# Key order for contiguous value weights in a two-layer attention kernel

## Chip, cores and metric

The kernel runs on one core of a Trainium2 chip. The metric is the device time of one execution in microseconds (us); where runs are compared, it is the median. The profile is of one execution. Everything is computed in float32.

## What is computed

The input x has shape (4, 32, 32, 768): four images of 1024 tokens and 768 channels. Two layers follow each other. Each normalises its input over 32 groups of channels, computes multi-head attention with 12 heads of 64 channels and a decomposed relative-position bias, projects the result and adds it to the input.

```python
def _gn(v, G=32, eps=1e-5):            # over height, width and the group's channels
    g = v.reshape(B_, H_, W_, G, C_ // G)
    return ((g - m) / jnp.sqrt(s + eps)).reshape(v.shape)
# attention of one layer, S = 1024 tokens
qkv = x @ Wqkv                          # layer 1 adds qkv_b
rel_h = jnp.einsum('bhwc,hkc->bhwk', r_q, Rh)
rel_w = jnp.einsum('bhwc,wkc->bhwk', r_q, Rw)
bias = rel_h[..., :, None] + rel_w[..., None, :]
attn = jax.nn.softmax(scale * jnp.einsum('bqc,bkc->bqk', q, k) + bias, axis=-1)
out = jnp.einsum('bqk,bkc->bqc', attn, v)
x = x + (out @ Wproj + bproj)
```

A key token has a row y and a column x, its number being 32y + x. Its bias is the sum of a row entry and a column entry. The softmax and the weighted sum over keys do not depend on the order of the keys, as long as scores, biases and values use the same one.

## The kernel before

**Units.** There are 8 images (4 for each layer) of 6 head pairs, so 48 head pairs `g`, and each has 8 steps `n` of 128 query tokens. Channels lie on the partitions in x (`xn`, six chunks of 128), queries and keys; tokens do in values.

**Work of a head pair.** `project_in` (L201) multiplies the normalised input by the query and key weights, 512 tokens at a time: ScalarE copies one half of the sum out of PSUM and VectorE (DVE) adds the other (L226 to L229). `project_values` (L236) does the values of two head pairs in four quarters; there the weights that TensorE loads are tokens of `xn`, 128 for one of 8 planes, and the rows that stream are the weight matrix (L248 to L252). `positions` (L268) multiplies queries with the tables of relative positions, and `diagonals` (L294) reads the needed entries back from DRAM into `rel`.

**Work of a step.** `biases` (L311) adds row and column entries on GpSimd (POOL) into a tile `sc` of 128 queries x 1024 keys, two steps ahead. `scores` (L321) multiplies queries by keys, subtracts in one VectorE instruction (L337) with the row's extreme, and takes the exponential on ScalarE (L341). `divide` (L346) rescales on GpSimd (L351). `turn` (L353) transposes 32 x 32 blocks on VectorE (L365) and writes them to DRAM (`td`); `read_back` (L373) fetches them as `pt`, with the keys on the partitions. Each of the 8 planes `k` of `pt` holds 128 keys. `weigh` (L381) multiplies the planes of `pt` with those of the values, twice a head pair. The order of keys decides which tokens a plane holds: before, keys stand in order 32x + y, and a plane holds every eighth token, so L250 takes its weights at a step of eight elements.

**Order.** All of it is one program written out by hand (`manual_schedule`). In each step `biases`, `scores`, `turn` and `divide` come at fixed places, and slices of projections for the next head pair and of the output projection fill the rest: `take` (L516) takes `shares[n]` slices of a list `todo`. A slice of the output projection (`project_out`, L462) is one matmul of 512 columns; a group of one to three slices ends with an eviction on VectorE (L481, L483). An fp32 matmul stands as two instructions in the trace. `early` and `later` hold calls that are issued one or two steps on, and `fetch` (L422) asks for output weights and residuals, four parts ahead. Loads and stores go through the queue of SyncE (SPq), save that ScalarE's queue (ACTq) writes `tdr` (L287) and, at the end, asks for the last `pt`. The group statistics of an image (`norm`, L156) pass through DRAM four times in small transfers: gather (L170), by_group (L173), back (L186) and spread (L189).

**PSUM.** Scores have two tiles (`ps_s`), everything else shares two others (`ps_m`), so a third group waits for the eviction of the first.

Of the kernel before, what the change touches and what calls it, by code (L numbers as in the profile page):

```python
# [36 lines left out]
P = 128  # L37
# [17 lines left out]
def attention_blocks(ctx: ExitStack, tc: tile.TileContext, a: dict, out: bass.AP):  # L55
# [100 lines left out]
    def norm(im):  # L156

        per = dram2.tile([C, 2], FP, tag="per", name=f"per_{im}")
        back = dram2.tile([C, 2], FP, tag="back", name=f"back_{im}")
        g = small.tile([NG, 2, GS, 2], FP, tag="g", bufs=1, name=f"g_{im}")
        st = small.tile([NG, 2, 6], FP, tag="gst", bufs=1, name=f"gst_{im}")
        mv = small.tile([NG, 3, 2], FP, tag="gmv", bufs=1, name=f"gmv_{im}")
        nrm = small.tile([P, NC, 2], FP, tag="nrm", bufs=2, name=f"nrm_{im}")

        def gather():
            nc.sync.dma_start(out=per.rearrange("(c p) s -> p c s", p=P), in_=mv_of[im])  # L170

        def by_group():
            nc.sync.dma_start(out=g[:, 0, :, :], in_=per.rearrange("(g k) s -> g k s", k=GS))  # L173

        def groups():
            for k in range(2):
                nc.vector.bn_stats(st[:, k, :], g[:, 0, :, k])
                nc.vector.bn_aggr(mv[:, k, :], st[:, k, :])
            nc.vector.tensor_scalar(mv[:, 2, 0:1], mv[:, 0, 1:2], mv[:, 1, 0:1], EPS, ALU.add, ALU.add)
            nc.scalar.activation(mv[:, 2, 1:2], mv[:, 2, 0:1], AF.Sqrt)  # L180

        def inverses():
            nc.vector.reciprocal(mv[:, 2, 0:1], mv[:, 2, 1:2])
            for k, x in enumerate((mv[:, 0, 0:1], mv[:, 2, 0:1])):
                nc.vector.tensor_copy(g[:, 1, :, k], x.to_broadcast([NG, GS]))
            nc.sync.dma_start(out=back.rearrange("(g k) s -> g k s", k=GS), in_=g[:, 1, :, :])  # L186

        def spread():
            nc.sync.dma_start(out=nrm, in_=back.rearrange("(c p) s -> p c s", p=P))  # L189
# [11 lines left out]
    def project_in(g, which, i):  # L201
# [16 lines left out]
                yield True  # L218
        to, t = qk_of[g, which], [t[:, a, :] for a in range(2)]
        if which == 1:  # L220
            to = to.rearrange("p (x y) -> p x y", x=HW)[:, :, i * HW // 2 : (i + 1) * HW // 2]
            t = [x.rearrange("p (y x) -> p x y", x=HW) for x in t]
        else:
            to = to[:, cols]
        if images[im][0] == 0:
# [10 lines left out]
    def project_values(g, i):  # L236
# [7 lines left out]
        for k in range(2):  # L244
            for c in range(NC):
                for a in range(2):
                    rows = slice(a * D, (a + 1) * D)
                    nc.tensor.matmul(  # L248
                        t[:, a, k, :],
                        lhsT=xn[c][rows, :].rearrange("p (m k) -> p k m", k=NT)[:, 2 * i + k, :],  # L250
                        rhs=w[rows, c, :], start=(c == 0), stop=(c == NC - 1),
                    )  # L252
                if c % 2 and (k, c) != (1, NC - 1):
                    yield True
# [56 lines left out]
    def biases(g, n):  # L311
        rel = rel_of[g]
        for h in range(2):
            sc = scpool.tile([P, HW, HW], FP, tag="sc", name=f"sc_{g}_{n}_{h}")
            sc_of[g, n, h] = sc
            nc.gpsimd.tensor_tensor(  # L316
                sc, rel[:, h, 1, n, :].unsqueeze(2).to_broadcast([P, HW, HW]),
                rel[:, h, 0, n, :].unsqueeze(1).to_broadcast([P, HW, HW]), ALU.add,
            )

    def scores(g, n):  # L321
# [11 lines left out]
        st = small.tile([P, 3, 2], FP, tag="sm", name=f"sm_{g}_{n}")  # L333
        st_of[g, n] = st
        for h in range(2):
            sc = sc_of[g, n, h].rearrange("p x y -> p (x y)")
            nc.vector.tensor_tensor_reduce(  # L337
                out=sc, in0=ps[h], in1=sc, scale=-scale, scalar=BIG, op0=ALU.add, op1=ALU.min,
                accum_out=st[:, 0, h : h + 1],
# [6 lines left out]
    def divide(g, n):  # L346
        st = st_of[g, n]
        nc.vector.reciprocal(st[:, 2, :], st[:, 1, :])  # L348
        for h in range(2):
            sc = sc_of[g, n, h].rearrange("p x y -> p (x y)")  # L350
# [22 lines left out]
    def read_back(g, quarter, h, td, queue=None):  # L373
# [1 line left out]
        pt_of[g, quarter, h] = pt  # L375
        (queue or nc.sync).dma_start(
            out=pt.rearrange("p r k t -> p r (k t)"),
            in_=td.rearrange("(r j) (y t) -> (j y) r t", r=4, y=4),
        )

    def weigh(g, quarters):  # L381
# [80 lines left out]
    def project_out(im, p, o, i):  # L462
# [26 lines left out]
        elif p == 2:  # L489
            nc.sync.dma_start(out=dst, in_=to)  # L490
        if i == 1 and (im, p, o, i) in place:
            (early if end else later).append(lambda: fetch(place[im, p, o, i] + 4))
        yield True


# [38 lines left out]
    with tc.manual_schedule(engines=ENGINES):  # L534
# [23 lines left out]
        for at, (g, n) in enumerate(units):  # L558
            im, pair = divmod(g, NP)
            end = im + 1 == NI  # L560
            if n == 0:
# [66 lines left out]
        take(todo, len(todo))  # L628

# [54 lines left out]
```

## Time and profile before

Time before: 3565.82 us median of 3 runs (3563.49 to 3567.86). The profiled execution took 3565.2 us. A row of the group table gives the busy time of all instructions of one line and kind, and the mean of one; PE is TensorE's matmuls and PEld its weight loads, which overlap them.

| line, engine | what | count | busy us | mean ns |
|---|---|---|---|---|
| L213 PE | query and key projection | 4608 | 1031.1 | 591 |
| L328 PE | scores | 3072 | 751.6 | 597 |
| L394 PE | weighted sum of values | 6144 | 687.4 | 381 |
| L248 PE | value projection | 4608 | 567.8 | 398 |
| L470 PE | output projection | 1080 | 477.3 | 598 |
| L316 POOL | bias sums | 768 | 1457.0 | 1918 |
| L351 POOL | rescaling | 768 | 852.0 | 1122 |
| L337 DVE | score minus bias | 768 | 909.6 | 1221 |
| L365 DVE | transposes | 768 | 909.9 | 1221 |
| L341 ACT | exponential | 768 | 879.1 | 1145 |

Matmuls overlap each other, so a busy time is less than count times mean. The DMA queue of SyncE keeps the 16 DMA engines busy for 81.8% of the span, that of ScalarE 4.2%.

### The profile page before, as it was taken

How to read it: one execution, taken by the hardware profiler on the slowest of the kernel's cores; microseconds unless marked ns; L12 is line 12 of the kernel's file. 1: busy time of each engine (PE TensorE's matmuls, PEld its weight loads, DVE VectorE, ACT ScalarE, POOL GpSimd, SP SyncE). 2: the span in 40 equal slices, each digit the busy share in tenths (PEclk: the TensorE clock that was granted, in tenths of full speed). 3: DMA queues.
4: the chain of work that ended last, by engine and by line, in shares of the span. 5: the costliest groups of instructions: out<-in, count | busy, mean ns of one | idle time of the engine just before them, and what ended most of it. 6: DMA issues, size and time to landing. Idle time of an engine off the chain costs nothing.

```text
span 3565.2 us, 55101 instructions
## 1 busy us (share of the span) xinstructions
PE 3515.4 (99%) x21120; PEld 2044.5 (57%) x21120; DVE 2381.5 (67%) x3676; ACT 1226.5 (34%) x2040; POOL 2297.6 (64%) x1546
## 2 busy tenths in 40 slices
PE   6999999999999999999999999999999999999998
PEld 4555565555655565556555565556555565556553
DVE  3676767767677666666766666666766667666665
ACT  2334333333333333333333333333333333333331
POOL 3767666666666666666666666666666666666663
PEclk9999999999999999999999999999999999999999
DMA  4889988998989888998989888898889898888886
GB/s 134 309 319 309 328 296 315 325 309 306 323 313 319 306 318 296 320 318 285 332 301 329 304 294 321 317 320 290 315 315 321 302 306 321 311 311 281 305 281 242
DMA packets 624856, 1084.53 MB, mean 304 GB/s; under 512 B 247120, under 2 KB 310096, under 8 KB 575440
## 3 DMA queue, kind: packets, MB, share of 16 engines
q1 hardware_dynamic: 570672, 1028.31, 81.8%
q10 hardware_dynamic: 53920, 52.70, 4.2%
q8 instruction: 166, 2.72, 0.3%
q14 instruction: 98, 0.80, 0.1%
HBM read 580.59 MB, written 500.27 MB: 303 GB/s over the span
## 4 chain that ended last, share of the span: by engine, by line
PE 96%; DMA 2%; DVE 1%; issue 0%; SPq 0%; ACT 0%; POOL 0%; DVEq 0%; ACTq 0%
PE pj L213 28%; PE s L328 19%; PE av L394 19%; PE pv L248 15%; PE o L470 14%; PE tp L280 3%; DMA tdr<-t 1%; DMA pt<-td 0%; DMA td<-tb 0%; DMA wv<-in_wv 0%; DVE tb L365 0%; SPq L306 0%; DVE sc L337 0%; DMA per<-mv 0%; SPq L94 0%
## 5 line engine op out<-in xcount | busy, mean ns | idle before, releaser
L351 POOL TENSOR_SCALAR sc<-sc,sm 128x1024 f32<-128x1024 f32 x768 | 852.0, 1122 | 1174.2 <-DVE sm L348 1161.0
L316 POOL TENSOR_TENSOR sc<-rel 128x1024 f32<-128x1024 f32 x768 | 1457.0, 1918 | 40.9 <-DMA rel<-tdr 40.9
L341 ACT ACTIVATE sc<-sc,sm 128x1024 f32<-128x1024 f32 x768 | 879.1, 1145 | 1377.8 <-DVE sm L337 1375.5
L337 DVE CUSTOM_DVE_ANT_0 sc<-s,sc 128x1024 f32<-128x1024 f32 x768 | 909.6, 1221 | 292.9 <-PE s L328 256.9
L213 PE MATMUL pj<-xn,w 64*128 64x512 f32 x4608 | 1031.1, 591 | 29.7 <-DVE xn L192 27.4
L365 DVE STREAM_TRANSPOSE tb<-sc 128x1024 f32<-128x1024 f32 x768 | 909.9, 1221 | 19.9 <-DMA td<-tb 19.0
L213 PEld LDWEIGHTS pj<-xn,w 64*128 64x128 f32 x4608 | 453.8, 188 | 568.7 <-issue 534.2
L328 PE MATMUL s<-k,q 64*128 64x512 f32 x3072 | 751.6, 597 | 7.4 <-DVE sm L337 7.3
L394 PE MATMUL av<-pt,v 128*64 128x256 f32 x6144 | 687.4, 381 | 4.6 <-DMA pt<-td 4.4
L394 PEld LDWEIGHTS av<-pt,v 128*64 128x64 f32 x6144 | 433.9, 137 | 287.6 <-ACT v L258 35.6
L248 PEld LDWEIGHTS pv<-wv,xn 64*128 64x128 f32 x4608 | 570.2, 331 | 31.1 <-DVE v L259 9.9
L248 PE MATMUL pv<-wv,xn 64*128 64x256 f32 x4608 | 567.8, 398 | 0.0
L470 PE MATMUL o<-attn,wo 128*128 128x512 f32 x1080 | 477.3, 598 | 0.0
L328 PEld LDWEIGHTS s<-k,q 64*128 64x128 f32 x3072 | 299.4, 188 | 291.3 <-issue 264.7
L470 PEld LDWEIGHTS o<-attn,wo 128*128 128x128 f32 x1080 | 202.2, 191 | 272.6 <-issue 262.1
L259 DVE TENSOR_TENSOR v<-pv,v 128x256 f32<-128x256 f32 x192 | 81.5, 424 | 320.3 <-ACT v L258 320.3
L258 ACT COPY v<-pv 128x256 f32<-128x256 f32 x192 | 71.4, 372 | 380.6 <-PE pv L248 333.0
L285 ACT COPY t<-tp 128x1024 f32<-128x1024 f32 x96 | 97.2, 1012 | 249.2 <-PE tp L280 147.5
L341 ACT ACTIVATION_READ_ACCUMULATOR sc<-sc,sm 128x1 f32 x768 | 143.3, 187 | 0.0
L229 DVE TENSOR_TENSOR q<-pj,q 128x512 f32<-128x512 f32 x96 | 66.3, 691 | 105.1 <-ACT q L226 53.5
L229 DVE TENSOR_TENSOR k<-pj,k 128x512 f32<-128x512 f32 x96 | 66.1, 689 | 92.8 <-ACT k L226 46.7
L280 PEld LDWEIGHTS tp<-tab,q 64*128 64x128 f32 x1536 | 100.1, 188 | 40.0 <-issue 39.9
(34 smaller groups left out, 788.2 us busy)
## 6 DMA issues: line engine op xcount, KB each, us to landing
td<-tb SPq DMA_DIRECT2D x384, 1024.0 KB, 5.9
pt<-td SPq DMA_DIRECT2D x382, 1024.0 KB, 7.7
tdr<-t ACTq DMA_DIRECT2D x96, 512.0 KB, 6.4
w<-in_wqk SPq DMA_DIRECT2D x96, 384.0 KB, 7.1
rel<-tdr SPq DMA_DIRECT2D x760, 32.0 KB, 2.2
part<-res SPq DMA_DIRECT2D x84, 256.0 KB, 5.1
res<-part SPq DMA_DIRECT2D x84, 256.0 KB, 9.2
wv<-in_wv SPq DMA_DIRECT2D x24, 768.0 KB, 8.7
```

Of the source, the lines that this page charges most:

```text
L213: nc.tensor.matmul(t[:, a, :], lhsT=w[rows, c, :], rhs=xn[c][rows, cols], start=(c == 0), stop=(c == NC - 1),)
L229: nc.vector.tensor_tensor(to, t[1], to, ALU.add)
L248: nc.tensor.matmul(t[:, a, k, :], lhsT=xn[c][rows, :].rearrange("p (m k) -> p k m", k=NT)[:, 2 * i + k, :], rhs=w[rows, c, :], start=(c == ...
L280: nc.tensor.matmul(ps[:, h, j, :], lhsT=q[rows, at * P : (at + 1) * P], rhs=tabs[l][rows, :], start=True, stop=True,)
L316: nc.gpsimd.tensor_tensor(sc, rel[:, h, 1, n, :].unsqueeze(2).to_broadcast([P, HW, HW]), rel[:, h, 0, n, :].unsqueeze(1).to_broadcast([P, ...
L328: nc.tensor.matmul(ps[h][:, cols], lhsT=q[rows, n * P : (n + 1) * P], rhs=k[rows, cols], start=True, stop=True,)
L337: nc.vector.tensor_tensor_reduce(out=sc, in0=ps[h], in1=sc, scale=-scale, scalar=BIG, op0=ALU.add, op1=ALU.min, accum_out=st[:, 0, h : h + 1],
L341: nc.scalar.activation(sc, sc, AF.Exp, bias=st[:, 0, h : h + 1], scale=-1.0, accum_out=st[:, 1, h : h + 1],)
L351: nc.gpsimd.tensor_scalar(sc, sc, st[:, 2, h : h + 1], 1.0, ALU.mult, ALU.mult)
L365: nc.vector.transpose(tb[:, :, j, :], sc_of[g, n, h])
L394: nc.tensor.matmul(av[rows, at * 2 * P : (at + 1) * 2 * P], lhsT=v_of[g][:, k, rows], rhs=pt_of[g, quarter, h][:, :, k, :], start=(k == 0) ...
L470: nc.tensor.matmul(t, lhsT=wo_of[im, o, c], rhs=attn_of[im * NP + c][:, cols], start=(c == c0), stop=(c == c1 - 1),)
```

## The change

The keys are put into another order. `project_in` writes key token 4m + a to place 256a + m, with a from 0 to 3. A plane of `pt` then holds 128 neighbouring tokens, and `project_values` takes `xn` as it lies. `biases` makes its sums in the same order: place 256a + 8(k u) + l has row (k u) and column 4l + a, so the row entry is held over 8 elements while the column entries are read in runs of 8 at a step of four elements; before, the column entry was held over 32 while 32 row entries were read in a run.

Beside it, the first image's statistics go through ScalarE's queue; in the last image a load is issued where its slot becomes free and not a step later; and in the last head pair the slices are shared out differently, with some of them before the transposes, and the twelve that are left over run ahead of the last two weightings.

```diff
@@ norm
+        queue = nc.sync if im else nc.scalar
         def gather():
-            nc.sync.dma_start(out=per.rearrange("(c p) s -> p c s", p=P), in_=mv_of[im])
+            queue.dma_start(out=per.rearrange("(c p) s -> p c s", p=P), in_=mv_of[im])
...
@@ project_in
         if which == 1:
-            to = to.rearrange("p (x y) -> p x y", x=HW)[:, :, i * HW // 2 : (i + 1) * HW // 2]
-            t = [x.rearrange("p (y x) -> p x y", x=HW) for x in t]
+            to = to.rearrange("p (a m) -> p a m", a=4)[:, :, i * P : (i + 1) * P]
+            t = [x.rearrange("p (m a) -> p a m", a=4) for x in t]
@@ project_values
-                        lhsT=xn[c][rows, :].rearrange("p (m k) -> p k m", k=NT)[:, 2 * i + k, :],
-                        rhs=w[rows, c, :], start=(c == 0), stop=(c == NC - 1),
+                        lhsT=xn[c][rows, (2 * i + k) * P : (2 * i + k + 1) * P], rhs=w[rows, c, :],
+                        start=(c == 0), stop=(c == NC - 1),
@@ biases
+            shape = [P, 4, HW, 8]
             nc.gpsimd.tensor_tensor(
-                sc, rel[:, h, 1, n, :].unsqueeze(2).to_broadcast([P, HW, HW]),
-                rel[:, h, 0, n, :].unsqueeze(1).to_broadcast([P, HW, HW]), ALU.add,
+                sc.rearrange("p (a k) (u l) -> p a (k u) l", a=4, l=8),
+                rel[:, h, 0, n, :].unsqueeze(1).unsqueeze(3).to_broadcast(shape),
+                rel[:, h, 1, n, :].rearrange("p (l a) -> p a l", a=4).unsqueeze(2).to_broadcast(shape),
+                ALU.add,
             )
@@ project_out
         if i == 1 and (im, p, o, i) in place:
-            (early if end else later).append(lambda: fetch(place[im, p, o, i] + 4))
+            if end:
+                fetch(place[im, p, o, i] + 4)
+            else:
+                later.append(lambda: fetch(place[im, p, o, i] + 4))
@@ the loop over units, last head pair of the last image
-                        shares = [0, 6, 6, 6, 6, 2, 0, 4]
+                        shares = [6, 6, 0, 6, 6, 2, 0, 4]
...
-            if n == NT - 1:
-                take(todo, share // 4)
-                share -= share // 4
+            first = 3 if n == NT - 1 else 2 if end and pair == NP - 1 and n in (3, 4) else 0
+            first = min(first, share)
+            take(todo, first)
+            share -= first
             turn(g, n)
@@ after the loop
-        run(early)
-        run(later)
-        weigh(NPAIR - 1, (2,))
-        while todo:
-            take(todo, 1)
-            run(early)
-            run(later)
-        weigh(NPAIR - 1, (3,))
+        take(todo, 12)
+        for quarter in (2, 3):
+            weigh(NPAIR - 1, (quarter,))
```

The other three transfers of the statistics change queue in the same way, and the softmax's views are renamed without moving anything.

More of the change, by code (lines that the diff above doesn't have):

```diff
@@ L167, in norm @@
         nrm = small.tile([P, NC, 2], FP, tag="nrm", bufs=2, name=f"nrm_{im}")
+        queue = nc.sync if im else nc.scalar
         def gather():
-            nc.sync.dma_start(out=per.rearrange("(c p) s -> p c s", p=P), in_=mv_of[im])
+            queue.dma_start(out=per.rearrange("(c p) s -> p c s", p=P), in_=mv_of[im])
         def by_group():
-            nc.sync.dma_start(out=g[:, 0, :, :], in_=per.rearrange("(g k) s -> g k s", k=GS))
+            queue.dma_start(out=g[:, 0, :, :], in_=per.rearrange("(g k) s -> g k s", k=GS))
         def groups():
@@ L185, in inverses @@
                 nc.vector.tensor_copy(g[:, 1, :, k], x.to_broadcast([NG, GS]))
-            nc.sync.dma_start(out=back.rearrange("(g k) s -> g k s", k=GS), in_=g[:, 1, :, :])
+            queue.dma_start(out=back.rearrange("(g k) s -> g k s", k=GS), in_=g[:, 1, :, :])
         def spread():
-            nc.sync.dma_start(out=nrm, in_=back.rearrange("(c p) s -> p c s", p=P))
+            queue.dma_start(out=nrm, in_=back.rearrange("(c p) s -> p c s", p=P))
         def apply(c):
@@ L335, in scores @@
         for h in range(2):
-            sc = sc_of[g, n, h].rearrange("p x y -> p (x y)")
+            sc = sc_of[g, n, h].rearrange("p k j -> p (k j)")
             nc.vector.tensor_tensor_reduce(
@@ L349, in divide @@
         for h in range(2):
-            sc = sc_of[g, n, h].rearrange("p x y -> p (x y)")
+            sc = sc_of[g, n, h].rearrange("p k j -> p (k j)")
             nc.gpsimd.tensor_scalar(sc, sc, st[:, 2, h : h + 1], 1.0, ALU.mult, ALU.mult)
@@ L377, in read_back @@
             out=pt.rearrange("p r k t -> p r (k t)"),
-            in_=td.rearrange("(r j) (y t) -> (j y) r t", r=4, y=4),
+            in_=td.rearrange("(r j) (a t) -> (j a) r t", r=4, a=4),
         )
```

## Prediction

> **What bounds the kernel now.** I read the page's busy shares first, then the chain that ended last, then the groups of instructions, then TensorE's timeline in the middle, at the start and at the end.
>
> ```profile
> PE 3515.4 (99%) x21120; PEld 2044.5 (57%) x21120; DVE 2381.5 (67%) x3676; ACT 1226.5 (34%) x2040; POOL 2297.6 (64%) x1546
> ...
> PE 96%; DMA 2%; DVE 1%; issue 0%; SPq 0%; ACT 0%; POOL 0%; DVEq 0%; ACTq 0%
> ```
>
> TensorE is busy 99% and carries 96% of the chain. In the chain in order of time, one output-projection block comes round at 1053.15, 1125.95 and 1198.74 us: one head pair every 72.79 us, 48 of them. So time goes where TensorE's stream gets shorter, provided nobody else needs more than about 72 us a head pair. The groups say which blocks can shrink:
>
> ```profile
> L213 PEld LDWEIGHTS pj<-xn,w 64*128 64x128 f32 x4608 | 453.8, 188 | 568.7 <-issue 534.2
> L248 PEld LDWEIGHTS pv<-wv,xn 64*128 64x128 f32 x4608 | 570.2, 331 | 31.1 <-DVE v L259 9.9
> L248 PE MATMUL pv<-wv,xn 64*128 64x256 f32 x4608 | 567.8, 398 | 0.0
> ```
>
> (The third field after the first bar is the idle time before them.) The two weight loads have one shape, 64 rows by 128 columns. That of the value projection takes 331 ns, not 188, and the weight-load path is hardly ever idle before it (31.1 us over 4608, against 568.7): these matmuls follow their weight loads. The only difference in the code is that L250 picks every eighth token (a step of 32 bytes), where L214 reads 128 neighbours.
>
> ```profile
> 1017.10 5.32 PE L213 MATMUL pj<-xn,w 64*128 64x512 f32 x24
> 1022.25 1.88 PE L328 MATMUL s<-k,q 64*128 64x512 f32 x8
> ...
> 1029.12 5.90 PE L248 MATMUL pv<-wv,xn 64*128 64x256 f32 x48
> 1034.80 1.93 PE L328 MATMUL s<-k,q 64*128 64x512 f32 x8
> ```
>
> Start to next start, a query/key block of 24 x 512 columns takes 5.15 us; a value block of 48 x 256, the same number of columns, takes 5.68 (5.73 in layer 1, where one runs from 3431.30 to 3437.03).
>
> [...]The trace has 188 ns for all loads of 128 neighbouring columns (L213, L280, L328) and 331 for the stepped one.[...]
>
> **The change, part by part.**
>
> *Value weights contiguous (L250).* 24 groups of two head pairs x 4 quarters = 96 blocks. A block cannot go below the 5.15 us of the block with equal columns. It has 24 instructions more; the relative-position block (1004.62 to 1005.52 us, 16 instructions of 128 columns) needs 0.056 us an instruction, of which 128 columns at 5.15/(24x512) = 0.42 ns are 0.0536, so 0.0025 us an instruction, 0.06 a block at most. That block also shows that 188 ns loads keep up at one per 56 ns; the value block needs one per 107. So 5.15 to 5.21; I take 5.19 against a mean of 5.71: 0.52 x 96 = **50 us** (48 to 54). Nothing lies beside it that has to end first: TensorE never stops between 119 us and the last head pair.
>
> *Key order, softmax, transposes, reads back (L221, L336, L350, L378).* Same shapes and sizes. The key eviction reads PSUM at a step of 4 elements instead of 32 and writes runs of 128 instead of 16. Before, the stepped k eviction (ACT 584, DVE 689 ns) costs what the plain q one does (585, 691), so I take 0, hidden under TensorE anyway. Scores and the DRAM round trip have the same patterns: 0.
>
> *Bias sums (L316), 768 on GpSimd.* The row input was contiguous; now the column input is read in runs of 8 at a step of 16 bytes, against a broadcast row entry. Not in this trace: lower bound 1918 ns, unchanged.[...] I take 2.8 as an estimate. Upper bound: double, if the runs of 8 cost as well, 3.8. GpSimd now needs 16 x (1918 + 1122 ns) = 48.6 us of 72.8 a head pair; at 2.8 it needs 62.8, still under TensorE's 71.75. Step by step: its idle times before L351 in one head pair are 0.91, 1.79, 3.94, 1.16, 6.34, 1.90, 4.35 and 4.77 us, and two sums become 1.8 us longer, so a rescale comes at most 0.9 us later. In the timelines the rescaled tile waits some 2 us or more for its transpose: rescale ended 1024.43, transposes began 1026.82, behind the scores' reduction. A sum made at 1006.76 to 1010.54 is first read at 1017.41. So hidden, except at the start: the first two sums (from 58.65 us) stand before the first reduction, **+1.4 us** (0 to 1.8), and about 2 at the very end, counted below.
>
> *First group statistics on ScalarE's queue.*
>
> ```profile
> 13.43 0.21 DVE L154 BATCH_NORM_AGGREGATE mv<-st 128x2 f32<-128x12 f32 x1
> 13.74 0.33 SPq L139 DMA_DIRECT2D bqkv<-in_bqkv  x1
> 15.75 0.38 SPq L170 DMA_DIRECT2D per<-mv  x1
> ```
>
> The statistics are there at 13.64, but the gather goes out at 15.75, and the queue's waits name the landing of wv for it. In a queue of its own it goes at about 13.7. The chain behind it (20.02, 23.10, 24.44, normalising at 26.50, first matmul 27.37) keeps its lengths: **-2 us** (0 to 2.5). Behind the gather on ScalarE stand only L180, which needs its result, and the first eviction at 35.65: no one waits longer. For images 1 to 7 nothing changes.
>
> *Last head pair.* Starts of the score blocks in steps 0 to 6 of before: 3465.76, 3469.16, 3480.88, 3495.46, 3504.85, 3514.23, 3518.06. These 52.3 us hold six score blocks (1.9 each), 26 output slices (24 instructions are 12 slices in 10.5 us, so 0.875) and one weighting of 7.06: 41.2 us of work, 11.1 lost. Step 0 has nothing to fill it while the scores wait for DVE to empty their PSUM tile; in steps 3 and 4 the third group waits 1.86 and 1.84 for DVE:
>
> ```profile
> 3469.16 4.92 PE L328 MATMUL s<-k,q 64*128 64x512 f32 x8 [1.41 <-DVE sm L337]
> ...
> 3502.94 1.99 PE L470 MATMUL o<-attn,w_last 128*128 128x512 f32 x4 [1.86 <-DVE sum L483]
> ...
> 3534.98 5.35 PE L394 MATMUL av<-pt,v 128*64 128x256 f32 x30 [2.45 <-DMA pt<-td]
> ```
>
> The new shares fill step 0 (step 2 has the weighting to fill it), and two slices ahead of the transposes let DVE empty one group before them: I give back 9 of 11.1, since DVE needs some 6.6 us of the 7.15 of such a step. After step 7, 3527.76 to 3561.4 = 33.6 us hold 22 slices (19.3), two half weightings (7.1) and one eviction (0.6): 6.7 lost, mostly waiting for pt (0.45 + 2.45 and a slow stretch after it). Twelve slices (10.5 us) ahead of both weightings cover the first pt. The last pt was asked for at 3540.0 and takes 7.7 to land; with three slices before the last transposes it comes some 1.5 us later, and the slower bias sum adds 2, so some of it shows: 4 back. **-13 us** in all (6 to 18). The fetch in place makes the sync queue wait for a residual buffer with td writes and pt reads behind it; 0, since a DVE eviction frees it within a group of three slices (2.6 us), and the queue's waits show td writes held up 52 times, by up to 2.9 us, without TensorE waiting.
>
> Sum: 3565.8 - 50 + 1.4 - 2 - 13 = 3502.2 us.
>
> **The rivals.** *GpSimd becomes the bound.* It passes 72.8 us a head pair at 72.8/16 - 1.12 = 3.43 us a sum, between my bounds. At 3.8 it needs 16 x 4.92 = 78.7: 48 x 78.7 + 58.7 before its first sum + some 30 after its last rescale = 3866 us, slower by 8%. For it: runs of 8, a read never seen here, and the engine already at 64%.[...] Chance 12%. *GpSimd shows in part*, at 3.1 to 3.4 us a sum: 67 to 72 us a head pair, with short steps in which it no longer catches up; a third to three quarters of the gain goes, 3520 to 3550. Chance 10%. *The loads stay slow* (331 ns is not the step but a conflict on xn): only the edges remain, 3565.8 - 13.6 = 3552. Against it: q, read as weights at 128 neighbours, takes 188. Chance 4%. *DMA becomes the bound*: its share in the middle, 0.85 to 0.89, becomes 0.86 to 0.90, and the pt asked for at 1036.17 lands, at the median 7.7, about when the weighting at 1044.11 starts, which reads it 3.5 us later; if transfers stretch, half the gain goes, 3535. Chance 4%.
>
> **How the numbers follow.** The forecast has 70%; its unknowns (48 to 54, 0 to 1.8, 0 to 2.5, 6 to 18) reach from 3491 to 3514, wider by a little as I can't see inside the last pair. Up to 3545 the partial cases are in; left out are the GpSimd bound, 3552 and the ends. Faster by over 0.2%: 70 + 10 + 4 + 4 less 3 for partial losses that are worse than thought = 85%; within 0.2% 3%; slower 12%.
>
> **What would show it.** L248's weight loads at 188 ns with long idle times before them, value blocks of 5.15 to 5.2 us, a head pair in 71.7 to 71.8; L316 at 2.8 us with GpSimd near 87% of a head pair and TensorE still at 99%; first matmul at about 25.3; no wait at L470 for sum and 16 us or less from step 0's lost time at the end. I am wrong if L316 passes 3.4 us, or if TensorE waits for DVE's reduction in the middle.

## The result, and the profile after

The changed kernel takes 3507.93 us (median of 4 runs, 3507.25 to 3508.77), the kernel before, timed beside it, 3564.65 (3560.87 to 3567.86). The ratio is 0.9841, with a 95% interval of 0.9824 to 0.9858: 56.7 us less. The forecast was 3502.

The page of the changed kernel, first its busy shares, then the chain by engine:

```profile
PE 3462.3 (99%) x21120; PEld 1921.4 (55%) x21120; DVE 2381.1 (68%) x3676; ACT 1227.5 (35%) x2040; POOL 2729.9 (78%) x1546
...
PE 97%; DMA 2%; DVE 0%; SPq 0%; issue 0%; ACT 0%; POOL 0%; ACTq 0%; DVEq 0%
```

TensorE is still the bound. The two engines that moved are TensorE, 53 us less, and GpSimd, 432 us more, which the chain does not feel. The groups behind them (after the second bar: idle time before, and its releaser):

```profile
L319 POOL TENSOR_TENSOR sc<-rel 128x1024 f32<-128x1024 f32 x768 | 1890.4, 2485 | 38.2 <-DMA rel<-tdr 38.2
...
L249 PE MATMUL pv<-wv,xn 64*128 64x256 f32 x4608 | 515.7, 376 | 0.0
L249 PEld LDWEIGHTS pv<-wv,xn 64*128 64x128 f32 x4608 | 448.3, 187 | 90.8 <-issue 30.1
```

The value weights load in 187 ns instead of 331, and their matmuls hold TensorE 52 us less. A bias sum takes 2485 ns instead of 1918. TensorE's timeline in the middle:

```profile
1013.66 5.32 PE L214 MATMUL pj<-xn,w 64*128 64x512 f32 x24
1018.81 5.35 PE L249 MATMUL pv<-wv,xn 64*128 64x256 f32 x48
1023.99 1.88 PE L333 MATMUL s<-k,q 64*128 64x512 f32 x8
```

From start to next start a value block now takes 5.18 us (5.68 to 5.73 before), next to 5.15 for the query/key block with the same number of columns.

The two profiled executions (3565.2 and 3507.0 us) can be set beside each other at marks that TensorE passes in both. All marks are starts in its timeline.

| stretch | before, us | after, us | difference |
|---|---|---|---|
| start to first matmul | 27.37 | 25.73 | -1.6 |
| to the first weighting of the second head pair | 158.94 | 160.68 | +1.7 |
| to the scores in step 0 of the last head pair | 3279.45 | 3231.70 | -47.8 |
| to the scores in step 6 of it | 52.30 | 42.12 | -10.2 |
| to the end | 47.2 | 46.8 | -0.4 |

So the middle gave what its blocks promised, and two stretches did not: the first head pair even grew, though it has shorter value blocks and starts sooner, and the last stretch hardly moved in this pair of executions, though twelve slices had been put where TensorE used to wait. The experiments ask about these, and about the margin under GpSimd.

One thing is needed for all of them. In the traces of both kernels the granted clock of TensorE is either full (1.00) or half (0.50), and half for 3.41 us at a time, once for 6.83. Such a stretch cost a busy TensorE half its length: the middle, as defined below, is 3212.2 us with one of 3.41 us in it and 3213.9 with two (changed kernel and best_of_both), 1.7 more. Up to the end of TensorE's work, the trace of before has 10.2 us at half clock (6.83 from 3470.28 us and 3.41 from 3535.14), that of the changed kernel 13.7 (from 122.93, 133.17, 198.02 and 3491.89).

### The profile page after: what moved, and what is told of

Read it like the earlier page. It is cut to its first block, busy times and chain, and to the rows that moved or that the text cites. A ratio compares the mean times of both kernels' runs of the same rounds, so it can differ in the third digit from the quotient of the medians.

```text
span 3507.0 us, 55102 instructions
## 1 busy us (share of the span) xinstructions
PE 3462.3 (99%) x21120; PEld 1921.4 (55%) x21120; DVE 2381.1 (68%) x3676; ACT 1227.5 (35%) x2040; POOL 2729.9 (78%) x1546
## 4 chain that ended last, share of the span: by engine, by line
PE 97%; DMA 2%; DVE 0%; SPq 0%; issue 0%; ACT 0%; POOL 0%; ACTq 0%; DVEq 0%
PE pj L214 28%; PE s L333 19%; PE av L399 19%; PE o L475 14%; PE pv L249 14%; PE tp L281 3%; DMA tdr<-t 1%; DMA pt<-td 1%; SPq L307 0%; DMA td<-tb 0%; DMA wo<-in_wo 0%; DMA xn<-in_x 0%; DVE st L152 0%; DMA rel<-tdr 0%; DMA per<-mv 0%
## 5 line engine op out<-in xcount | busy, mean ns | idle before, releaser
L319 POOL TENSOR_TENSOR sc<-rel 128x1024 f32<-128x1024 f32 x768 | 1890.4, 2485 | 38.2 <-DMA rel<-tdr 38.2
L342 DVE CUSTOM_DVE_ANT_0 sc<-s,sc 128x1024 f32<-128x1024 f32 x768 | 909.8, 1222 | 293.3 <-PE s L333 266.4
L333 PE MATMUL s<-k,q 64*128 64x512 f32 x3072 | 750.1, 598 | 7.0 <-DVE sm L342 6.9
L249 PE MATMUL pv<-wv,xn 64*128 64x256 f32 x4608 | 515.7, 376 | 0.0
L249 PEld LDWEIGHTS pv<-wv,xn 64*128 64x128 f32 x4608 | 448.3, 187 | 90.8 <-issue 30.1
L333 PEld LDWEIGHTS s<-k,q 64*128 64x128 f32 x3072 | 288.5, 187 | 299.5 <-issue 275.5
```

Of the source, the lines that this page charges most:

```text
L249: nc.tensor.matmul(t[:, a, k, :], lhsT=xn[c][rows, (2 * i + k) * P : (2 * i + k + 1) * P], rhs=w[rows, c, :], start=(c == 0), stop=(c == N ...
L319: nc.gpsimd.tensor_tensor(sc.rearrange("p (a k) (u l) -> p a (k u) l", a=4, l=8), rel[:, h, 0, n, :].unsqueeze(1).unsqueeze(3).to_broadcas ...
L333: nc.tensor.matmul(ps[h][:, cols], lhsT=q[rows, n * P : (n + 1) * P], rhs=k[rows, cols], start=True, stop=True,)
L342: nc.vector.tensor_tensor_reduce(out=sc, in0=ps[h], in1=sc, scale=-scale, scalar=BIG, op0=ALU.add, op1=ALU.min, accum_out=st[:, 0, h : h + 1],
```

## Experiments

A time "in the middle" is that of 45 head pairs, from the second's first weighting to the 47th's: 3260.0 us before, 3212.2 after.

### Which part brought the gain

`contig_only`: before, with the weights alone.

```diff
-    lhsT=xn[c][rows, :].rearrange("p (m k) -> p k m", k=NT)[:, 2 * i + k, :],
+    lhsT=xn[c][rows, (2 * i + k) * P : (2 * i + k + 1) * P],
```

> The kernel before, with one edit: the value projection takes 128 neighbouring tokens as weights. Keys, biases and probabilities keep their old order, so planes and values do not match and only the time is read. Theory A (the step of the weight loads was the cost): L248's loads fall from 331 to 187 ns, a value block from 5.73 to 5.18 us, a head pair from 72.8 to 71.7, so 48 x 1.1 = 53 us less: about 3512, ratio 0.985. Rival B (the key order as a whole, or the edges, brought the gain): within 5 us of before.

`order_only`: the changed kernel with the statistics' queue, the fetches, the shares and the end of before.

```diff
-        queue = nc.sync if im else nc.scalar
+        queue = nc.sync
...
-                        shares = [6, 6, 0, 6, 6, 2, 0, 4]
+                        shares = [0, 6, 6, 6, 6, 2, 0, 4]
```

> The changed kernel with its edges undone: the first statistics on the sync queue, the old shares, the old end and deferred fetches; only the order of keys, the bias sums and the value weights are new. Theory A: a head pair in 71.7 us; the dearer bias sums (2.49 for 1.92 us) cost nothing in the middle and 1 to 3 us at the start and the end, so 3513 to 3516, at most 4 us above the run with contiguous weights alone. Rival C (dearer bias sums eat part of the gain in the middle): 10 us or more above it and a head pair over 71.8 us.

`edges_only`: before with those edits, and the old order of keys.

```diff
+        queue = nc.sync if im else nc.scalar
...
-                        shares = [0, 6, 6, 6, 6, 2, 0, 4]
+                        shares = [6, 6, 0, 6, 6, 2, 0, 4]
```

> The kernel before with the other edits alone: first statistics on ScalarE's queue, new shares, slices ahead of the transposes, fetch in place, twelve slices ahead of the last two weightings. From the two traces: 1.6 us at the first matmul and some 10.6 us in the last head pair, so about 3552, ratio 0.9966. Rival: with the cheap bias sums the end gains the 3.6 us more that I had forecast (3548); if the edges and the order depend on each other, the sum of both parts misses the whole by over 4 us.

Measured beside the kernel before at 3562.24 us (3559.33 to 3568.07):

| kernel | median, us | ratio, 95% interval | middle, us | second head pair's first weighting, us |
|---|---|---|---|---|
| contig_only | 3519.77 | 0.9876 (0.9861 to 0.9891) | 3212.2 | 188.24 |
| order_only | 3518.85 | 0.9874 (0.9860 to 0.9889) | 3212.2 | 188.16 |
| edges_only | 3552.75 | 0.9970 (0.9958 to 0.9981) | 3260.0 | 185.33 |

Three things follow. The step of the weight loads is the whole of the middle's gain: with it gone alone, the middle takes exactly what it takes in the changed kernel. (In all three traces with the shorter blocks the middle holds one stretch of 3.41 us at half clock, in the two others none; at full clock a head pair goes from 72.79 to 71.69 us.) From which step on a load gets dear was not tried: 32 bytes and none are the two cases (331 and 187 ns), and why the step costs is not shown. The dearer bias sums cost nothing at all, not even at the start: both kernels reach the second head pair at 188.2 us, one with sums of 1918 ns and one with 2485. And the parts add up: 43.4 and 9.5 us are 52.9, and the whole, timed in another round, is 54.3 below the same 3562.24. The miss is that contig_only and order_only end at 3519 and not at 3512 to 3516. It lies at the start: they reach the second head pair 1.9 us later than before, where six shorter blocks should have brought them there 3 us sooner. Some 5 us go there, with cheap sums and dear ones alike: before the second half of the first weighting both wait longer for pt (contig_only 3.45 us, order_only 2.92, before 1.50), and both run two stretches of 3.41 us at half clock after it, the kernel before none.

### The statistics' queue

`stats_on_sync`: the changed kernel with `queue = nc.sync` for all images.

> The changed kernel with the first statistics back on the sync queue. If the earlier first matmul (25.73 for 27.37 us) goes through to the end: 1.6 us slower than the changed kernel, 3509.5. Rival: the first head pair is held by its transfers (the first weighting waits for pt), which hang on other requests, and the difference is under 0.5 us.

3508.88 us (3507.01 to 3512.06), against 3507.93 (3507.25 to 3508.77): the ranges overlap. The first matmul is at 27.34 us instead of 25.73, the second head pair's first weighting at 187.34 instead of 186.41. In this pair the queue is worth 1.6 us where it acts, 0.9 after the first head pair, and at the end no more than the spread. The 1.6 is itself one draw: in the traces here the first matmul stands at 25.43 to 26.91 us with ScalarE's queue and at 27.23 to 27.37 with the sync queue. What it is worth in the end stays open to about a microsecond.

### What the first head pair lost

TensorE in the first weighting, before:

```profile
119.25 4.10 PE L394 MATMUL av<-pt,v 128*64 128x256 f32 x34
124.85 3.67 PE L394 MATMUL av<-pt,v 128*64 128x256 f32 x30 [1.50 <-DMA pt<-td]
```

and in the changed kernel:

```profile
114.62 3.67 PE L399 MATMUL av<-pt,v 128*64 128x256 f32 x32
119.04 0.65 PE L399 MATMUL av<-pt,v 128*64 128x256 f32 x2 [0.74 <-DMA pt<-td]
122.66 5.35 PE L399 MATMUL av<-pt,v 128*64 128x256 f32 x30 [2.98 <-DMA pt<-td]
```

TensorE comes 4.6 us sooner and then waits 3.7 instead of 1.5; after the longer wait the same 30 instructions take 5.35 us instead of 3.67. The windows (busy time of each engine with instructions; clock, DMA share and GB/s last) show why: in the changed kernel the granted clock is at half for 3.41 us of each of these two, before in neither. Before, and then in the changed kernel:

```profile
120.00:130.00 10.00, 8.50 (x68) 4.83 (x64) 5.95 (x10) 2.39 (x4) 3.99 (x4) 1.00 0.98 374
130.00:140.00 10.00, 8.55 (x39) 3.52 (x38) 8.25 (x13) 4.75 (x8) 9.36 (x7) 1.00 1.03 398
```

```profile
120.00:130.00 10.00, 7.27 (x38) 3.68 (x38) 2.79 (x5) 0.00 (x0) 3.37 (x3) 0.83 0.99 395
130.00:140.00 10.00, 8.62 (x30) 3.65 (x32) 8.39 (x13) 4.75 (x8) 8.81 (x6) 0.83 1.05 401
```

So the 4.6 us by which TensorE comes sooner are lost again: 2.2 to the longer wait, and about 3.4 (estimate) to the two stretches at half clock, against 1.1 that the last two value blocks of the pair still gain. What held pt is in the sync queue's timeline of the changed kernel: 16 small reads of relative positions for the second head pair stand ahead of it and wait for their own data.

```profile
104.44 8.80 SPq L307 DMA_DIRECT2D rel<-tdr  x16
113.28 1.00 SPq L381 DMA_DIRECT2D pt<-td  x2
```

`start_read_first` asks for pt ahead of them, in the first head pair alone:

```diff
+            if g == 0:
+                run(behind)
             run(early)
```

> The changed kernel, with the first head pair's pt asked for ahead of the 16 relative-position reads of the next one on the sync queue. If those reads hold pt up and the first weighting's wait and the slow clock after it ate the start's gain: no wait at the first weighting (114.6 us), the clock stays at 1.0 from 120 to 140 us, the second head pair's first weighting falls from 186.4 to about 180, and the end by 5 to 6 us, 3502. Rival (the transfers themselves are late because the DMA engines are full): under 2 us.

```profile
102.48 3.14 SPq L381 DMA_DIRECT2D pt<-td  x2
108.29 9.34 SPq L307 DMA_DIRECT2D rel<-tdr  x16
```

3501.09 us (3499.75 to 3505.34), ratio 0.9821 (0.9806 to 0.9836): 6.8 us below the changed kernel by the medians. The first weighting runs through in this trace (117.89 us, 64 instructions in 7.13). The last of the pt reads now lands at 113.36 us and not at 122.62, so it would have been in time for a TensorE that comes at 114.62, too. The profiled execution is the slowest of the four; it reaches the second head pair at 183.42 and not at 180, since TensorE comes to the weighting later (117.89 for 114.62: it ran at half clock from 62.21 to 69.04 us), and the clock falls a step after it (0.83 from 130 to 140 us), where the next scores wait for their PSUM (1.43 us, ended by VectorE's reduction). So the request's place in the queue is shown to be the cause of the wait. It does not decide the clock, which was at half in one of the two windows in which I expected it not to be; so the size at the start differs from run to run by some microseconds.

### What a bias sum costs

`bias_forms`: eight ways of reading the second operand, chosen by step and head; only one of them is the changed kernel's, and the others add other entries.

```diff
+            form = 2 * (n % 4) + h
+            if form == 0:
+                add(sc, row32, rel[:, h, 1, n, :].unsqueeze(1).to_broadcast(wide), ALU.add)
+            elif form == 1:
+                add(out8, row8, rel[:, h, 1, n, :].rearrange("p (l a) -> p a l", a=4)...)
...
```

> The changed kernel with eight ways of reading the bias sums' second operand, one for each of (n mod 4, h), each on a line of its own; most of them add entries that do not belong together, so only the mean time of each line is read. Operand in runs of 32 at steps of 1, 2, 4 and 8 elements and broadcast (step 0), and in runs of 8 at steps of 1, 2 and 4. Known: runs of 32, step 1: 1918 ns; runs of 8, step 4: 2485. If the step is the cost[...]: steps 4 and 8 about 2485 whatever the runs, steps 0 to 2 about 1918. If the short runs are the cost: 2485 for all runs of 8 and 1918 for all runs of 32. If both share it, runs of 8 at step 1 and runs of 32 at step 4 lie between.

The groups of this kernel on GpSimd, the three dear forms and the three nearest to them:

```profile
L329 POOL TENSOR_TENSOR sc<-rel 128x1024 f32<-128x1024 f32 x96 | 241.3, 2513 | 0.0
L339 POOL TENSOR_TENSOR sc<-rel 128x1024 f32<-128x1024 f32 x96 | 236.3, 2462 | 0.0
L333 POOL TENSOR_TENSOR sc<-rel 128x1024 f32<-128x1024 f32 x96 | 233.4, 2431 | 0.0
L335 POOL TENSOR_TENSOR sc<-rel 128x1024 f32<-128x1024 f32 x96 | 192.3, 2003 | 0.0
L331 POOL TENSOR_TENSOR sc<-rel 128x1024 f32<-128x1024 f32 x96 | 187.4, 1952 | 0.0
L337 POOL TENSOR_TENSOR sc<-rel 128x1024 f32<-128x1024 f32 x96 | 187.0, 1948 | 0.0
```

| runs | step 0 | step 1 | step 2 | step 4 | step 8 |
|---|---|---|---|---|---|
| of 32 | 1907 (L341) | 1911 (L327) | 1948 (L337) | 2431 (L333) | 2462 (L339) |
| of 8 | | 1952 (L331) | 2003 (L335) | 2513 (L329) | |

(ns; a step of 4 elements is 16 bytes.) The step is the cost: with runs of 32, 8 bytes take 37 ns more than neighbouring elements, 16 bytes 483 more than 8, and 32 bytes 31 more than 16; runs of 8 add 41 to 82 ns. The kernel as a whole took 3503.58 us in one execution, 5.2 below the changed kernel's profiled one. Of that some 3.4 go with the clock, which is at half in two stretches of its trace and in four of the changed kernel's.

### How far GpSimd is from being the bound

`pool_more4` and `pool_more8` repeat a sum, in the first of odd steps only and in all.

```diff
-            nc.gpsimd.tensor_tensor(
+            for _ in range(2 if h == 0 and n % 2 else 1):     # pool_more8: if h == 0
+              nc.gpsimd.tensor_tensor(
```

> The changed kernel, with the first head's bias sum done twice in every odd step: GpSimd needs 57.8 + 4 x 2.49 = 67.7 us of a head pair's 71.7, as if a sum took 3.1 us. If GpSimd's work stays hidden until it fills the head pair: within 5 us of the changed kernel, a head pair still 71.7. If it shows in part, as my second rival had it (3520 to 3550 at 3.1 to 3.4 us a sum): 12 us or more above, with waits of TensorE for the scores' reduction in the middle.

> The same with the first head's bias sum done twice in every step: 57.8 + 8 x 2.49 = 77.7 us a head pair, as if a sum took 3.7 us. GpSimd is then the bound: 48 x 77.7 + 57 before the first sum + some 25 after the last = 3810, slower than before. Rival (GpSimd also loses time between its instructions, waiting for the reciprocal): a head pair over 79 us.

`pool_more4`: 3508.54 us (3507.66 to 3509.70), 0.6 above the changed kernel; a head pair has a median of 71.70. Its busy shares, and then the first two of TensorE's waits (us, how often, us of one):

```profile
PE 3460.0 (99%) x21120; PEld 1918.7 (55%) x21120; DVE 2401.9 (69%) x3676; ACT 1228.1 (35%) x2040; POOL 3203.4 (91%) x1738
```

```profile
PE pj L214 <- DVE xn L193: 25.7, 1, 25.7
PE s L334 <- DVE sm L343: 12.2, 10, 2.0
```

In the changed kernel the second of them is `PE s L333 <- DVE sm L342: 6.9, 6, 1.4`. 45 head pairs take 3215.7 us, 3.5 more than in the changed kernel (some 5.2 at the same clock, as here the middle has no stretch at half), for 10 us more of GpSimd in every one of them. All of it lies in the second and third head pairs, which have no output projection: they take 66.49 and 66.37 us for 65.51 (with one stretch at half clock) and 63.83, close to the 67.7 that GpSimd needs. From the fourth to the 46th each takes 71.69 or 71.70, as in the changed kernel. So even at 91% GpSimd's work is hidden wherever TensorE has 71.7 us to do, as much as with sums of 3.1 us on the mean (16 x 2485 + 4 x 2485 = 20 x 2485 = 16 x 3106 ns).

`pool_more8`: 3781.39 us (two runs, 3780.72 and 3782.05), ratio 1.0605 (1.0584 to 1.0626). Its busy shares, and GpSimd's group of sums (24 a head pair, written as 1152 in all):

```profile
PE 3577.2 (95%) x21120; PEld 1995.1 (53%) x21120; DVE 2415.0 (64%) x3676; ACT 1243.2 (33%) x2040; POOL 3660.3 (97%) x1930
```

```profile
L320 POOL TENSOR_TENSOR sc<-rel 128x1024 f32<-128x1024 f32 x1152 | 2827.8, 2470 | 67.8 <-DMA rel<-tdr 37.6
```

A head pair now takes 77.02 us at the median, and GpSimd's own work in it is 24 x 2.470 + 16 x 1.134 = 77.4 (a little over 77.02, as neighbouring sums overlap in the trace: 1152 of 2470 ns are 2845 us, for 2827.8 busy). It has become the bound, at no more than its own work; 3810 us had been expected, with 77.7 a head pair. So the limit for one sum is about 71.7/16 - 1.13 = 3.35 us, an estimate. At 2.49 GpSimd needs 16 x (2.485 + 1.127) = 57.8 of 71.7 us, 81%.

### What the end lost

TensorE in the last stretch of the changed kernel, from the twelve slices on:

```profile
3475.55 9.43 PE L475 MATMUL o<-attn,w_last 128*128 128x512 f32 x20 [0.20 <-DVE sum L488]
3484.91 4.10 PE L399 MATMUL av<-pt,v 128*64 128x256 f32 x34
3491.42 5.35 PE L399 MATMUL av<-pt,v 128*64 128x256 f32 x30 [2.40 <-DMA pt<-td]
3497.35 5.80 PE L475 MATMUL o<-attn,w_last 128*128 128x512 f32 x12 [0.58 <-DVE attn L411]
```

The wait has not gone; it has moved. Before (the prediction shows the line at 3534.98 us), it stood ahead of the first of the two weightings, now ahead of the second, with the same two costs: some 2.4 us idle, and 30 instructions in 5.35 us instead of 3.67. The windows show what else runs there:

```profile
3475.55:3484.90 9.35, 9.35 (x20) 3.30 (x20) 5.39 (x8) 0.00 (x0) 0.00 (x0) 1.00 0.99 339
3484.90:3491.40 6.50, 4.11 (x35) 2.48 (x34) 1.17 (x2) 0.00 (x0) 0.00 (x0) 1.00 0.98 372
3491.42:3497.00 5.58, 5.35 (x30) 2.96 (x30) 0.19 (x1) 0.00 (x0) 0.00 (x0) 0.69 0.03 10
```

DMA is full (0.99, 0.98) until the last pt is there at 3491.37, and then empty, and the clock is 0.69. That pt was asked for at 3481.33 us and took 10.0; before, the same request went out at 3539.96 and landed at 3545.69, in 5.7 (the prediction had taken the median of such reads, 7.7). What is new is six stores of the output: they go out from 3480.87 to 3485.74, since the twelve slices that produce them have moved ahead. Before, the first went out at 3547.30, after the last pt had landed. Three runs take this apart.

`tail_stores_late` puts these six stores behind both weightings in the program:

```diff
+        elif p == 2 and i == 0:
+            early.append(lambda: nc.sync.dma_start(out=dst, in_=to))
...
         for quarter in (2, 3):
             weigh(NPAIR - 1, (quarter,))
+        run(early)
```

> The changed kernel, with the six output stores of the twelve slices issued after both last weightings and not before them. If these stores (6 x 256 KB, 1.5 MB, some 4.5 us at the 340 GB/s of this stretch) hold up the last pt: the wait of 2.40 us before the last weighting and the slow clock after it (30 instructions in 5.35 us for 3.3) go, 3 to 4.4 us at the end, 3504. Rival (pt is late because its transposes and its own round trip are late): under 1 us.

3507.73 us (3506.64 to 3508.75), ratio 0.9838 (0.9825 to 0.9852): no change. The sync queue in its timeline:

```profile
3481.93 5.20 SPq L495 DMA_DIRECT2D out<-sum  x6
3497.96 5.01 SPq L497 DMA_DIRECT2D out<-sum  x6
```

The six stores left as early as ever: the last was out by 3487.13 us, and the second weighting, which stands ahead of them in the program, began at 3491.84. The queue that issues them waited for their sums and for nothing that TensorE did later, so their place in the program did not hold them. The run says nothing about the stores.

`tail_turn_first` takes two slices away from ahead of the last transposes, so that td is written sooner:

```diff
-            first = 3 if n == NT - 1 else 2 if end and pair == NP - 1 and n in (3, 4) else 0
+            first = (1 if end and pair == NP - 1 else 3) if n == NT - 1 else 2 if end and pair == NP - 1 and n in (3, 4) else 0
```

> The changed kernel, with one slice instead of three ahead of the last transposes, as before the change. The last transposes then start right after the evictions of the weighted sum, 1.6 us sooner. If the last pt is late because of its transposes: 1.6 us less wait and less of the slow clock, 2 to 3.5 us, 3505. Rival (the stores hold it up): under 1 us.

3510.05 us (3508.83 to 3511.21), ratio 0.9845 (0.9831 to 0.9858). The transposes begin 8.0 us after the weighting of step 6 instead of 9.7, but the last td lands 18.7 us after it, not 18.4, and the last pt 28.0, not 28.5. An earlier request gained next to nothing where DMA was full already (0.98 from 3484.90 to 3491.40 us); the three slices ahead of the transposes were not the loss. (The whole is 2.1 us slower for its start: in the profiled execution the clock is at half for 13.7 us before the second head pair, which comes at 190.38 us.)

`stores_held`: the six stores really wait. ScalarE copies the last weighted sum out of PSUM instead of VectorE, then one column of each sum's tile, and then issues its store in its own queue. The start of `start_read_first` is in it too.

```diff
-                nc.vector.tensor_scalar(to[:, q], av[:, q], bqkv[:, 2, pair : pair + 1], None, ALU.add)
+                if g == NPAIR - 1 and quarters[0] == 3:
+                    nc.scalar.activation(to[:, q], av[:, q], AF.Identity, bias=bqkv[:, 2, pair : pair + 1])
...
+        elif p == 2 and i == 0:
+            def store():
+                nc.scalar.copy(to[:, :1], to[:, :1])
+                nc.scalar.dma_start(out=dst, in_=to)
+            early.append(store)
```

> The changed kernel with pt ahead of the position reads in the first head pair, and the six stores truly held: ScalarE evicts the last weighted sum, touches one column of each of the six tiles after that, and then issues their stores (in the run before, the sync queue sent them out early all the same, at 3481.9 us). In the traces the last pt lands 28.5 us after the start of step 6's weighting with the stores in flight, 25.0 without them (kernel before), and TensorE is there after 25.6. If the stores take its DMA time: no wait before the last half weighting, clock 1.0 after it, start of that weighting to the end some 4 us shorter than the changed kernel's 44.1, total about 3497. If the DMA engines are filled by td and pt alone: 43 to 44 us and 3501.

```profile
3482.91 7.13 PE L399 MATMUL av<-pt,v 128*64 128x256 f32 x64
3490.61 5.80 PE L478 MATMUL o<-attn,w_last 128*128 128x512 f32 x12 [0.57 <-ACT attn L412]
```

Now both weightings run through as one block of 64 instructions, and they do so at full clock. The last pt was asked for at 3479.01 and landed at 3485.89, in 6.9 us instead of 10.0. From the weighting of step 6 to the end it takes 40.5 us, where the changed kernel takes 44.1 and start_read_first 43.6. So the stores' traffic is what held pt: shown, and not by this pair alone. In the changed kernel and in all nine other runs with the new last part in which the six stores go out beside it the last pt takes 9.0 to 10.3 us. How much of the 3.6 us this is worth is another matter, since the changed kernel's trace is at half clock for 3.41 us there. Five other executions with the same last part stay at full clock (stats_on_sync, bias_forms, tail_stores_late, edges_only, pool_more4): they wait 0.75 to 1.76 us for pt and take 41.1 to 41.8 us from the weighting of step 6 to the end. Against these, holding the stores is worth 0.6 to 1.3 us. The run also moved an eviction to ScalarE, but that eviction comes behind the wait and costs the same (0.57 for 0.58).

`best_of_both` is start_read_first with the edits of tail_stores_late and tail_turn_first.

> The changed kernel with pt ahead of the position reads in the first head pair, one slice ahead of the last transposes, and the six stores late. If the three are independent: some 6.8 us from the start (3501.1 for 3507.9) and 4.4 at most from the end, so 3496 to 3498, faster than both kernels. Rival: the end gives nothing, 3501.

It takes 3502.29 us, not 3496 to 3498, and still waits 2.64 for the last pt, since its six stores leave early, too (from 3475.25 us). These are the versions that beat both kernels, beside the changed one:

| kernel | median, us | range | ratio, 95% interval | second head pair's first weighting, us | step 6's weighting to the end, us |
|---|---|---|---|---|---|
| changed kernel | 3507.93 | 3507.25 to 3508.77 | 0.9841 (0.9824 to 0.9858) | 186.41 | 44.1 |
| start_read_first | 3501.09 | 3499.75 to 3505.34 | 0.9821 (0.9806 to 0.9836) | 183.42 | 43.6 |
| best_of_both | 3502.29 | 3498.91 to 3504.53 | 0.9823 (0.9809 to 0.9836) | 179.04 | 42.7 |
| stores_held | 3502.89 | 3500.11 to 3503.16 | 0.9827 (0.9814 to 0.9841) | 184.41 | 40.5 |

All three lie below the changed kernel, and their ranges overlap. That stores_held saves 3 us at the end and has no lower median than start_read_first fits the clock: its profiled execution reaches the second head pair 1 us later and is still 2.2 us shorter (3503.16 for 3505.34), but the three other executions of start_read_first were granted 0.999 on the mean and all five of stores_held 0.998, and 0.001 of 3500 us is 3.5 us. The start varies by some 5 us between these three, which share its code, and that is the clock: before the second head pair best_of_both has no stretch at half clock, the two others 10.2 us each (from 62 and 131 us), which cost some 5.1. Taken off as half of their length (an estimate), the second head pair would come at 178.3 to 179.3 us in these three, and at 182.6 to 184.0 in the changed kernel, bias_forms, tail_stores_late and tail_turn_first, where pt is asked for late. So the request alone is worth some 3 to 6 us. Why the clock falls in one execution and not in another stays open.

## Why the prediction was right, and where it was wrong

**Value weights: right.** 5.19 us a block were forecast, 5.18 measured; the weight loads take 187 ns and now have 90.8 us of idle time before them, not 31.1. 45 head pairs hold 90 of the 96 blocks and became 47.8 us shorter, 0.53 a block against 0.52 forecast (0.55 at the same clock). A head pair takes 71.70 us (71.7 to 71.8 forecast).

**Bias sum: the cost was mis-sized, the verdict held.** 2.8 us were estimated, 2.485 measured. The 2.8 was the author's estimate, with no read at this step in the trace of before. The sum became 30% dearer (1918 to 2485 ns), and `bias_forms` shows 27% for the step alone (1911 to 2431). "Hidden" was right, and with more room than the estimate had. "Except at the start: +1.4" was wrong: contig_only and order_only reach the second head pair at the same time.

**Statistics' queue: right where it acts.** First matmul 1.6 us sooner in the profiled pair, 2 forecast; from run to run 0.3 to 1.9.

**"Nothing lies beside it that has to end first: TensorE never stops between 119 us and the last head pair": the step that failed.** Of 0.52 x 96, six blocks belong to the first head pair, and of those and the queue's 2 us nothing arrived: start to the second head pair is 186.41 us, before 186.31. The reading of the trace was wrong: before, TensorE stops for 1.50 us for pt in the weighting that begins at 119.25 us, and for 1.43 us ahead of the scores at 131.86, 196.79 and 261.72. TensorE got to the first of these 4.6 us sooner, but pt was asked for only 2.4 us sooner, being behind 16 reads in the sync queue; the wait grew to 3.7 us, and two stretches of 3.41 us at half clock followed. Where pt went first, the total was 6.8 us lower by the medians.

**Last head pair: -13 forecast, -10.6 in the profiled pair.** The first part, "I give back 9 of 11.1", brought 10.2. But some 3.4 of the 11.1 were clock, not missing slices: the trace of before is at half clock from 3470.28 to 3477.11 us, right after its wait of 1.41, and so are contig_only and order_only at the same place, the changed kernel not. The second, "Twelve slices ahead of both weightings cover the first pt ... some of it shows: 4 back", brought 0.4. That is in part a matter of luck: from the weighting of step 6 to the end the changed kernel's profiled execution takes 44.1 us for 44.6 before, and 41.1 to 41.8 in the five executions with the same last part and full clock. The cause named there, a later request, was not the main one: with the transposes 1.7 us sooner, pt landed 0.5 sooner (tail_turn_first). The term left out is the DMA time of the slices' own stores, which now lie beside the read of the last pt (stores_held); it is worth 0.6 to 1.3 us at full clock, and the rest is the longer wait of this one execution and the half clock after it.

**The rivals.** GpSimd as the bound exists as described, from some 3.35 us a sum on (the prediction's 3.43 fills the old head pair of 72.8 us), and pool_more8 shows its price; the sum itself is 0.86 us short of it. Of the partial loss between 3.1 and 3.4 us (3520 to 3550) little shows at its lower end: at 91% of GpSimd the middle lost 3.5 us of 3212, in two head pairs alone, and the total 0.6. Loads that stay slow: 187 ns. DMA as the bound does not appear in the middle (the head pair has its forecast length), but a wait for a transfer is what both failed steps have in common.

The sum: 63.6 us were forecast and 58.2 came in the profiled pair, 56.7 in the medians. The middle gave 47.8 where 0.52 x 90 = 46.8 were due. The start gave nothing of some 3.7 (3.1 for six blocks and 2 for the queue, less 1.4), and the end 2.4 too little. Some microseconds of this are the clock's doing in these two executions: 10.2 us at half clock before, 13.7 after.

## What to carry to other kernels

Compare weight loads of one shape with each other. Here one took 331 ns and another 188, with 31.1 us of idle time in the load path before 4608 of the first and 568.7 before as many of the second: the matmuls followed the slow loads, and the operand's step was a cost that its layout could take away (187 ns after). When the bounding engine gets faster, look at each wait for a transfer that it now reaches sooner, first at what stands ahead of that transfer in its queue. The gain of the first head pair was lost there: 2.2 us to the longer wait, and some 3.4 (estimate) to the half clock after it. Work moved ahead to cover a wait brings its own transfers along: with six stores beside it the last pt took 10.0 us, without them 6.9. And these stores were held back by what they depend on in their queue, not by their place in the program: put behind both weightings, they left from 3481.93 us all the same.

## What the runs showed of the hardware

- A GpSimd add of 1024 elements with one input at a step took 1948 ns at 8 bytes, 2431 at 16 and 2462 at 32 (`bias_forms`, runs of 32). I had expected it to follow the step or the runs of 8; runs of 8 added only 41 to 82 ns.
- A weight load of 64 x 128 elements took 331 ns at a step of 32 bytes and 187 ns from neighbouring elements, and a block of 48 matmuls of 256 columns behind such loads took 5.68 to 5.73 us in the one case and 5.18 in the other.
- In the traces of both kernels the granted clock fell to 0.50, and to no other value, for 3.41 us at a time, once for 6.83; within one such stretch 30 instructions took 5.35 us for 3.67. While TensorE worked, every such stretch in these two traces began 0.2 to 1.8 us after the end of a stop of TensorE of over 1 us, whether that was for pt or for VectorE: before from 3470.28 and 3535.14 us, after stops that end at 3469.16 and 3534.98; in the changed kernel from 122.93, 133.17, 198.02 and 3491.89, after stops that end at 122.66, 131.36, 196.89 and 3491.42. Not every stop was followed by one: the changed kernel's stop of 1.43 us that ends at 262.39 was not, nor were tail_turn_first's of 1.91 and best_of_both's of 2.64 at the end, while start_read_first's of 1.93 at the same place was. What decides is open.
